# Selective scans on one Trainium2 core: taking a job's sum out and beginning the next one step apart, with additions up to three steps later

## The chip, the cores and the metric

The kernel is one program on one core of a Trainium2 chip. The metric is its device time in microseconds (us), given as the median of several executions. The core has five engines with an instruction queue each: TensorE (PE; its weight loads appear as PEld), VectorE (DVE), ScalarE (ACT), GpSimd (POOL) and SyncE (SP), which here only issues DMA transfers. They run side by side and wait for one another through semaphores.

## The reference, cut to what matters

Four layers work on an image batch of 2 x 56 x 56 x 128 in 32-bit floats. Layers 0 and 1 hold four-direction selective scans; layers 2 and 3 are attention, a spectral mixer and experts, which the change does not touch. What one scan computes, for each direction k (rows forward, columns forward, and both backward), channel d and time l:

```python
def step(state, inp):
    u_i, d_i, b_i, c_i = inp
    dA = jnp.exp(d_i[..., None] * A)
    state = dA * state + (d_i * u_i)[..., None] * b_i[:, :, None, :]
    y = jnp.einsum('bkdn,bkn->bkd', state, c_i)
    return (state, y)
```

There are 16 states n for each channel, and the output y at a time is the sum over them of state times c. The four directions are then added at each pixel. Layer 0 has 256 channels for each of two images. Layer 1 scans 64 channels of both images together, one head after another, four heads.

## The kernel before, in words

Channels lie on the 128 partitions, the 3136 pixels along the free dimension, in four quarters of 784 (`QT`). A *group* is a direction kd and a quarter q; the order of directions is 0, 2, 1, 3: rows forward, rows backward, columns forward, columns backward. A *job* is a group and a block of 128 channels (`nch` is 2 in layer 0, 1 in layer 1). A job has 16 *steps*, one for each state n. There are six runs of the scans: two of 512 steps in layer 0 (one for each image), four of 256 in layer 1 (one for each head), 2048 steps and 128 jobs in all.

For a step the work passes from engine to engine:

- ScalarE: `decay` (L334), a = exp(delta x A), into one of two PSUM buffers; `keep` (L345) saves the last column of a finished scan for the next quarter.
- TensorE: `spread` (L359) puts row n of the input matrix on all partitions, b, in a single PSUM buffer (pool `prow`). The same buffer is used by the preparation's products (L161).
- VectorE: the product h = du x b (L412), then the scan itself (L353), in place in h. For five of the 16 states (`POOLED`: 2, 5, 8, 11, 14) GpSimd makes the product (L428), from a b that a DMA has put on all partitions.
- GpSimd: the output product p = h x c (L425), with c brought by a DMA.
- TensorE: `add_up` (L373) adds p to the job's sum `acc` in PSUM with an identity matrix, two matmuls, each of which appears as two passes in the profile.

A job's sum is begun by `begin_sum` (L387): TensorE writes into `acc` what y holds for this quarter from the earlier directions, or, for kd 0, the direct term. After the 16th addition `take_out` (L393) copies `acc` back to y on ScalarE, in two copies. There is one `acc` buffer, so a job's begin waits for the take-out of the job before. `y_half` (L364) gives the place in y: for kd 1 and 3 its elements are one image row, 56 elements, apart.

The order of all instructions is written by hand: `emit(s)` issues, for every s, parts of several steps, and each engine takes its own in that order. At s it issues the decay of step s+1, `keep` of s-1, VectorE's product of s+1, the spread of s+2, a preparation's matmuls (`prepare(s, 0)`), the scan of s, the fetches of c for s+3 and of b for s+6, GpSimd's p of s and product of s+3, and then TensorE's additions. A step with n is done, for the additions, two values of s later. Before the change take_out stands first on ScalarE at the s where the new job's step 2 is scanned, and begin_sum last on TensorE at the same s; steps 0 to 7 of a job are then added three values of s after their scan, 8 to 15 two after it.

`preparation` (L252 on) makes delta, du and the bands of later groups while a job runs. Its lists give a step offset for each piece over two jobs, which I call a pair; the jobs of a pair are the first and second. In layer 0: `rows` at 0 and 3, `steps` at 12 and 16, `soft` (softplus, with a change of ScalarE's table before and after it) at 20, `copy` and `times` (du, L218) at 22 and 25. In layer 1 (after its first job): `rows` at 0 and 6, `steps` at 3 and 16, `soft` at 20, `copy` and `times` at 22 and 25. Offset 16 is step 0 of the second job. The last pair of a run has no preparation.

Of the kernel before, what the change touches and what calls it, by code (L numbers as in the profile page):

```python
# [30 lines left out]
NS = 16  # L31
# [74 lines left out]
class Scans:  # L106
# [30 lines left out]
    def open(self, ctx):  # L137
        k, nch = self.k, self.nch
        self.once = ctx.enter_context(k.pool("scan4", 1))
        self.two = ctx.enter_context(k.pool("scan5", 2))  # L140
        self.hp = ctx.enter_context(k.pool("scanh", 6))
        self.pp = ctx.enter_context(k.pool("scanp", 4))
        self.cp = ctx.enter_context(k.pool("scanc", 4))
        self.bp = ctx.enter_context(k.pool("scanb", 2))
        self.dram = ctx.enter_context(k.tc.tile_pool(name="scand", bufs=4, space=bass.MemoryType.DRAM))
        self.pa = [ctx.enter_context(k.pool(f"pdec{i}", psum=True)) for i in range(2)]
        self.pb = ctx.enter_context(k.pool("prow", psum=True))
        self.pc = ctx.enter_context(k.pool("psum", psum=True))
# [154 lines left out]
    def all_steps(self):  # L303
        steps, self.pieces = [], {}

        more = 2 // self.nch
        sets = [self.groups[:1]] + [self.groups[i : i + more] for i in range(1, len(self.groups), more)]
        for i, groups in enumerate(sets):
            for t in self.preparation(sets[i + 1], i == 0) if i + 1 < len(sets) else []:
                self.pieces.setdefault((len(steps) + t[0], t[1]), []).append(t)  # L310
            for g in groups:
                for ci in range(self.nch):
                    job = dict(g=g, ci=ci)
                    steps += [dict(job=job, g=g, ci=ci, n=n, s=len(steps) + n) for n in range(NS)]
        self.state = {}
        self.steps = steps
        for s in range(-6, len(steps) + 4):
            self.emit(s)
# [78 lines left out]
    def emit(self, s):  # L397
        nc = self.k.nc
        now, one, two, three = (self.at(s + i) for i in range(4))
        before, done, out = self.at(s - 1), self.at(s - 2), self.at(s - 3)  # L400
        if s == len(self.steps) + 2:
            self.take_out(self.steps[-1]["job"])
            return
        if out and out["n"] == NS - 1 and done:
            self.take_out(out["job"])
        if one:
            self.decay(one)
        if before:
            self.keep(before)
        if one and one["n"] not in POOLED:  # L410
            one["h"] = self.hp.tile([128, QT], F32, name="h")
            nc.vector.tensor_tensor(one["h"], one["g"]["du"][one["ci"]], one["b"], ALU.mult)  # L412
        if two and two["n"] not in POOLED:
            self.spread(two)
        self.prepare(s, 0)
        if now:
            self.scan(now)
        far = self.at(s + 6)
        if far and far["n"] in POOLED:
            far["b"] = self.on_all(self.bp, far["g"], "b", far["n"])  # L420
        if three:
            three["c"] = self.on_all(self.cp, three["g"], "c", self.w["rowC"] + three["n"])
        if now:
            now["p"] = self.pp.tile([128, QT], F32, name="p")
            nc.gpsimd.tensor_tensor(now["p"], now["h"], now["c"], ALU.mult)  # L425
        if three and three["n"] in POOLED:
            three["h"] = self.hp.tile([128, QT], F32, name="h")
            nc.gpsimd.tensor_tensor(three["h"], three["g"]["du"][three["ci"]], three["b"], ALU.mult)  # L428

        if done and done["n"] == 0:  # L430
            self.begin_sum(done["job"])
        elif done:
            if done["n"] <= 8:
                self.add_up(out)
            if done["n"] >= 8:
                self.add_up(done)
        self.prepare(s, 2)


# [1547 lines left out]
```

## Time and profile before

Times of three executions: 9255.02, 9247.24 and 9253.21 us; median 9253.21. The profiled execution took 9254.57, with a span of 9252.7.

| Engine | busy, us | share of the span |
|---|---|---|
| PE (matmul) | 8116.6 | 88% |
| DVE | 7112.8 | 77% |
| POOL | 6326.5 | 68% |
| ACT | 3840.2 | 42% |

| Scan run | first scan, us | last scan ends, us |
|---|---|---|
| layer 0, image 0 | 116.0 | 1388.8 |
| layer 0, image 1 | 1523.6 | 2795.1 |
| layer 1, head 0 | 2956.4 | 3598.4 |
| layer 1, head 1 | 3707.0 | 4345.9 |
| layer 1, head 2 | 4454.5 | 5097.2 |
| layer 1, head 3 | 5205.3 | 5844.4 |

How to read the profile's lines: a group has its line in the kernel (L412), engine and operation, out<-in, the shapes and the number of instructions; then busy us, mean ns of one, and the idle time of the engine just before them with what ended most of it. In the rows of slices each digit is the busy share of one fortieth of the span in tenths. A wait line has who waited for whom, the us in total, how often, and the longest. A timeline line has start and length in us, engine, instruction, and in brackets the engine's idle time before it and what ended it. TensorE's matmuls are pipelined and their ends are modelled, so the distance from one start to the next says more than their length.

### The profile page before, as it was taken

What the parts mean: (1) busy time and instruction counts of PE and PEld (TensorE: products, weight loads), DVE (VectorE), ACT (ScalarE), POOL (GpSimd) and SP (SyncE); (2) the same over time, 40 slices, a digit from 0 to 9 for tenths busy, and PEclk for the clock granted to TensorE, in tenths of its full rate; (3) what the DMA queues carried; (4) which work ended last, traced back from release to release, by engine and by line L of the source; (5) the groups of instructions that cost most, each with busy time, mean ns of one, the idle gap of its engine ahead of it and who ended that gap; (6) DMA issues with size and microseconds to landing.
All of it is one profiled execution on the core that took longest, in us unless ns stands there. A gap on an engine that the chain in (4) does not pass through costs nothing.

```text
span 9252.7 us, 94254 instructions
## 1 busy us (share of the span) xinstructions
PE 8116.6 (88%) x28825; PEld 4759.4 (51%) x28825; DVE 7112.8 (77%) x7587; ACT 3840.2 (42%) x6553; POOL 6326.5 (68%) x4023
## 2 busy tenths in 40 slices
PE   7888888888888888888888888599999999999998
PEld 3444445444444444444444444355588888874555
DVE  8999998999995997998899799711376676665442
ACT  4555545555544555554555555333211111114331
POOL 5999996999994996998799699666411111115551
PEclk9999999999998998999999899699999999999998
DMA  5666663666663885896688488200233333320003
GB/s 155 224 222 215 213 213 120 223 224 218 213 214 87 227 224 134 216 228 171 174 225 222 124 230 222 65 3 3 64 110 94 106 101 96 103 62 7 14 5 128
DMA packets 781381, 1364.59 MB, mean 147 GB/s; under 512 B 133213, under 2 KB 406494, under 8 KB 780842
## 3 DMA queue, kind: packets, MB, share of 16 engines
q1 hardware_dynamic: 780874, 1358.56, 51.2%
q8 instruction: 229, 3.75, 0.2%
q14 instruction: 278, 2.28, 0.1%
HBM read 1318.63 MB, written 39.60 MB: 147 GB/s over the span
## 4 chain that ended last, share of the span: by engine, by line
PE 54%; DVE 23%; issue 12%; ACT 5%; POOL 4%; DMA 1%; SPq 0%; DVEq 0%; POOLq 0%; ACTq 0%
PE cv L1515 13%; DVE h L353 11%; PE acc L373 11%; DVE h L412 7%; PE av L1027 5%; PE sc L1033 5%; PE pj L1629 4%; PE b L161 3%; PE acc L387 2%; PE b L359 2%; PE pcv L454 1%; ACT a L334 1%; POOL p L425 1%; POOL h L428 1%; PE cv L1577 1%
## 5 line engine op out<-in xcount | busy, mean ns | idle before, releaser
L425 POOL TENSOR_TENSOR p<-h,c 128x784 f32<-128x784 f32 x2048 | 3758.3, 1860 | 158.9 <-PE acc L373 91.5
L373 PE MATMUL acc<-p,ident 128*128 128x392 f32 x8192 | 3113.5, 509 | 181.3 <-POOL p L425 178.4
L353 DVE TENSOR_TENSOR_SCAN h<-a,state,h 128x784 f32<-128x784 f32 x1536 | 2794.4, 1843 | 35.7 <-POOL h L428 16.2
L373 PEld LDWEIGHTS acc<-p,ident 128*128 128x128 f32 x8192 | 1489.4, 194 | 1298.5 <-POOL p L425 372.6
L412 DVE TENSOR_TENSOR h<-du,b 128x784 f32<-128x784 f32 x1408 | 1339.6, 951 | 172.8 <-PE b L359 170.0
L334 ACT ACTIVATE a<-delta,L0A 128x784 f32<-128x784 f32 x1024 | 939.7, 919 | 864.0 <-DVE h L353 862.0
L334 ACT ACTIVATE a<-delta,L1A 128x784 f32<-128x784 f32 x1024 | 939.3, 919 | 826.8 <-DVE h L353 824.9
L428 POOL TENSOR_TENSOR h<-du,b 128x784 f32<-128x784 f32 x640 | 1188.6, 1857 | 2.9 <-DMA b<-rows 2.9
L359 PE MATMUL b<-three,sel 96*128 96x512 bf16 (+1 forms) x2816 | 703.7, 331 | 379.8 <-DVE h L412 338.6
L1046 POOL TENSOR_TENSOR total<-total,e 128x448 f32<-128x448 f32 (+1 forms) x644 | 734.4, 1140 | 326.1 <-ACT e L1035 286.4
L353 DVE TENSOR_TENSOR_SCAN h<-a,h 128x784 f32<-128x784 f32 x512 | 901.8, 1780 | 26.2 <-ACT a L334 15.5
L1528 DVE TENSOR_TENSOR u<-u,cv 128x512 f32<-128x512 f32 x1024 | 624.0, 684 | 326.5 <-PE cv L1515 325.3
L1559 POOL TENSOR_TENSOR u<-u,S 128x1024 f32<-128x1024 f32 x64 | 150.1, 2367 | 1043.8 <-DVE S L1528 1028.4
L359 PEld LDWEIGHTS <-sel 96*128 96x128 bf16 x2816 | 277.8, 99 | 974.4 <-issue 781.5
L1035 ACT ACTIVATE e<-sc 128x448 f32<-128x448 f32 (+1 forms) x700 | 376.9, 542 | 725.6 <-PE sc L1033 594.5
L1530 ACT COPY u<-cv 128x512 f32<-128x512 f32 x256 | 149.2, 586 | 827.3 <-PE cv L1515 773.7
L1629 PE MATMUL pj<-u,Wm 128*128 128x196 f32 (+8 forms) x1536 | 354.2, 384 | 5.7 <-DVE A L1635 5.7
L1033 PE MATMUL sc<-big 128*128 128x448 f32 (+1 forms) x700 | 323.5, 548 | 12.1 <-ACT e L1035 12.1
L1027 PE MATMUL av<-e,big 128*128 128x448 f32 (+1 forms) x700 | 320.8, 545 | 1.2 <-DVE e L1040 1.1
L1609 POOL TENSOR_TENSOR both<-mpm 128x512 f32<-128x512 f32 x32 | 40.6, 1269 | 390.0 <-DVE Wm L1665 271.7
L1629 PEld LDWEIGHTS pj<-u,Wm 128*128 128x128 f32 x1536 | 268.4, 192 | 71.3 <-issue 46.0
L972 DVE TENSOR_REDUCE m<-lo 112x1 f32<-112x448 f32 x392 | 229.3, 618 | 95.1 <-PE lo L968 94.9
(438 smaller groups left out, 10805.4 us busy)
## 6 DMA issues: line engine op xcount, KB each, us to landing
c<-rows SPq DMA_DIRECT2D x1024, 392.0 KB, 4.0
c<-rows SPq DMA_DIRECT2D x2048, 196.0 KB, 4.6
b<-rows SPq DMA_DIRECT2D x320, 392.0 KB, 4.6
b<-rows SPq DMA_DIRECT2D x640, 196.0 KB, 4.5
H<-raw SPq DMA_DIRECT2D x32, 1568.0 KB, 7.5
wC<-win SPq DMA_DIRECT2D x64, 576.0 KB, 6.2
w<-in_L_weight_dram SPq DMA_DIRECT2D x52, 512.0 KB, 5.3
wA<-win SPq DMA_DIRECT2D x64, 384.0 KB, 5.4
```

What stands on the lines that cost most here:

```text
L334: self.k.nc.scalar.activation(x["a"], g["delta"][ci], AF.Exp, scale=self.w["A"](g["kd"], ci, x["n"]))
L353: self.k.nc.vector.tensor_tensor_scan(h, a, h, start, ALU.mult, ALU.add)
L359: self.k.nc.tensor.matmul(ps[:, c0:c1], lhsT=self.w["selB"](x["n"]), rhs=x["g"]["three"][:, c0:c1], start=True, stop=True)
L373: nc.tensor.matmul(job["acc"][:, i, 0:392], lhsT=self.k.ident, rhs=x["p"][:, 392 * i : 392 * (i + 1)], start=False, stop=n == NS - 1,)
L412: nc.vector.tensor_tensor(one["h"], one["g"]["du"][one["ci"]], one["b"], ALU.mult)
L425: nc.gpsimd.tensor_tensor(now["p"], now["h"], now["c"], ALU.mult)
L428: nc.gpsimd.tensor_tensor(three["h"], three["g"]["du"][three["ci"]], three["b"], ALU.mult)
L1027: nc.tensor.matmul(acc, lhsT=V[b][:n, j, :], rhs=e[:n], start=j == 0, stop=j == NKT - 1)
L1033: nc.tensor.matmul(ps[:n], lhsT=keys[b][:, KT * j : KT * j + n], rhs=q, start=True, stop=True)
L1046: nc.gpsimd.tensor_tensor(total[:n], total[:n], e[:n], ALU.add)
L1515: self.k.nc.tensor.matmul(ps[:, b], lhsT=v[:, C * b : C * (b + 1)], rhs=h, start=i == 0, stop=i == len(terms) - 1)
L1629: nc.tensor.matmul(ps[:, lo - c0 : hi - c0], lhsT=Ws[f][:, eo, r, :], rhs=u[:, b, f, lo - a0 : hi - a0], start=f == 0, stop=f == 1,)
```

## The change

A finished job's take-out moves one value of s later, to where step 3 of the next job is scanned, and behind the decay instead of ahead of it. The begin of the next job's sum moves two values later, to step 4. The additions go through a list, `self.sums`: done steps are put in, the first is taken out one value of s after the begin, and at the done steps 6, 9 and 12 two are added in place of one, so that the list is empty again at the job's end. Until then an addition comes up to five values of s after its scan. The pool of output products p has six buffers in place of four.

```diff
-        self.pp = ctx.enter_context(k.pool("scanp", 4))
+        self.pp = ctx.enter_context(k.pool("scanp", 6))
...
-        self.state = {}
+        self.state, self.sums = {}, []
...
     def emit(self, s):
         nc = self.k.nc
         now, one, two, three = (self.at(s + i) for i in range(4))
-        before, done, out = self.at(s - 1), self.at(s - 2), self.at(s - 3)
+        before, done = self.at(s - 1), self.at(s - 2)
         if s == len(self.steps) + 2:
             self.take_out(self.steps[-1]["job"])
             return
-        if out and out["n"] == NS - 1 and done:
-            self.take_out(out["job"])
         if one:
             self.decay(one)
+        if done and done["n"] == 1 and done["s"] > NS:
+            self.take_out(self.at(done["s"] - 2)["job"])
         if before:
             self.keep(before)
...
-        if done and done["n"] == 0:
-            self.begin_sum(done["job"])
-        elif done:
-            if done["n"] <= 8:
-                self.add_up(out)
-            if done["n"] >= 8:
-                self.add_up(done)
+
+        if done:
+            self.sums.append(done)
+            if done["n"] == 2:
+                self.begin_sum(done["job"])
+            elif done["n"] > 2:
+                for _ in range(2 if done["n"] in (6, 9, 12) else 1):
+                    self.add_up(self.sums.pop(0))
         self.prepare(s, 2)
```

## The prediction

> **What bounds the kernel now.** I read the page's table of engines and its costliest groups first, then the clock and the waits stretch by stretch, then one job boundary in the order of time.
>
> ```profile
> DVE  8999998999995997998899799711376676665442
> POOL 5999996999994996998799699666411111115551
> ...
> L425 POOL TENSOR_TENSOR p<-h,c 128x784 f32<-128x784 f32 x2048 | 3758.3, 1860 | 158.9 <-PE acc L373 91.5
> L373 PE MATMUL acc<-p,ident 128*128 128x392 f32 x8192 | 3113.5, 509 | 181.3 <-POOL p L425 178.4
> L353 DVE TENSOR_TENSOR_SCAN h<-a,state,h 128x784 f32<-128x784 f32 x1536 | 2794.4, 1843 | 35.7 <-POOL h L428 16.2
> L412 DVE TENSOR_TENSOR h<-du,b 128x784 f32<-128x784 f32 x1408 | 1339.6, 951 | 172.8 <-PE b L359 170.0
> ```
>
> The change touches only the six scan runs (two of 512 steps, four of 256; 116 to 5844 us, with other work between them). In them VectorE works nine tenths of the time. The starts of its scans give 39.78 us for a job of 16 steps in layer 0 and 40.09 in layer 1, of which 1.43 and 1.71 are idle. So VectorE's own work is 38.4 us a job, and GpSimd's, counted the same way, is 38.7 (layer 0) and 39.1 (layer 1). Both are near their limits; what can be won is VectorE's idle time, above all the 170.0 that L412 waits for the rows that TensorE spreads. Sorted by step, 126 of these stand at one place: before the product of step 6. The waits of VectorE in the column directions (kd 1, 3) of the first run, 744 to 1389 us:
>
> ```profile
> DVE h L412 <- PE b L359: 34.7, 14, 3.4
> ```
>
> and in its row directions (kd 0, 2), 160 to 744 us:
>
> ```profile
> DVE h L353 <- ACT a L334: 5.6, 8, 0.8
> ...
> DVE h L412 <- PE b L359: 0.2, 1, 0.2
> ```
>
> So the stall belongs to jobs whose sum begins with a strided read of y. One such job, first of a pair, in the timeline (start, length, engine):
>
> ```profile
> 827.32 1.62 ACT L393 COPY pair<-acc 128x392 f32<-128x392 f32 x2 [1.56 <-PE acc L373]
> 828.99 3.13 PE L387 MATMUL acc<-pair,ident 128*128 128x392 f32 x4 [1.37 <-ACT pair L393]
> 831.94 2.79 PE L161 MATMUL b<-big,xp 128*128 128x392 f32 x4
> 834.77 0.48 ACT L173 COPY xd<-b 128x392 f32<-128x392 f32 x1 [4.09 <-PE b L161]
> 836.04 0.50 PE L359 MATMUL b<-three,sel 96*128 96x512 bf16 x2
> 836.34 1.85 POOL L425 TENSOR_TENSOR p<-h,c 128x784 f32<-128x784 f32 x1 [1.59 <-PE acc L373]
> 836.64 0.97 DVE L412 TENSOR_TENSOR h<-du,b 128x784 f32<-128x784 f32 x1 [3.37 <-PE b L359]
> ```
>
> TensorE waits for take_out, begins the sum (four passes 0.72 apart, 2.95 in all; a contiguous begin takes 1.42), makes the prepared rows, which keep the one buffer of b until ScalarE has copied them, and only then spreads step 6: the product is 3.37 late. The rows took 0.65 a pass in place of 0.33. Two stretches of this boundary (length; busy time of TensorE, its weight loads, VectorE, ScalarE, GpSimd; granted clock; DMA share; GB/s):
>
> ```profile
> 828.20:831.40 3.20, 2.41 (x4) 0.90 (x5) 3.18 (x3) 2.48 (x6) 3.20 (x3) 1.00 0.75 266
> 831.50:834.80 3.30, 3.30 (x6) 1.58 (x5) 1.77 (x2) 0.03 (x1) 3.25 (x2) 0.50 0.56 216
> ```
>
> The throttle halved TensorE's clock just there, as it does after nearly every strided begin.
>
> **What the Trainium skill says.** TensorE: Matmul & The Clock Gate, Part 1 (What's actually happening): the clock is halved after a window of about 3.4 us with too little activity, windows running freely. The trace agrees: half-clock stretches of 3.41 us, each after a window in which TensorE was mostly below half busy or read strided. SBUF — State Buffer, Door 1, note on cachelines: strided reads pay once a step leaves a 16-byte line; the trace's 0.72 against 0.33 agrees, and 0.72 stays 0.72 at half clock, so that a strided begin loses nothing to the throttle. ScalarE: Activation LUTs, What ACT_TABLE_LOAD costs: 1283 ns a load; the trace has 1283. Perfetto Trace Analysis, Optimization Strategy: a bubble that repeats can mean too few buffers; GpSimd's 91.5 for the four buffers of p are such bubbles.
>
> **The change, part by part.** In step numbers n of the new job:
>
> *take_out moves from n=2, ahead of a(3), to n=3, behind a(4).* The same two copies (next instruction 1.4 us after the first, strided). In the job above a(3) no longer waits; a(4) starts when scan(2) ends, 828.85; take_out runs 829.7 to 831.1, the state copy to 831.25. Behind it stand the copy of the rows and a(5), which must wait for scan(3)'s end (831.45) anyway. Cost nothing.
>
> *The begin moves from n=2 to n=4, behind the spread of step 6.* First of a pair: h(4) ends at 829.66, rows on TensorE at 829.7, their copy 1.63 later (as at this job's step 0) at 831.3, done 831.8; spread of 6 at 831.9; scan(4) ends at 833.27: h(6) on time with 0.7 to spare. Begin 832.25 to 835.2; spread of 7; its product can start 0.6 later, 835.8. VectorE, not delayed now, wants it at 835.9 (h(6) 0.95 and scan(5) 1.8 after 833.27). That is just in time at full clock. But TensorE does little from n=2 to 4 now (no additions), so I expect a half-clock window at or near the begin: on the rows it adds 1.31 and makes step 6 about 0.7 late, on the spread of 7 it adds 0.33. In layer 1 the preparation there is steps (copy 0.91 in place of 0.48), 0.4 tighter. Bounds 0 to 1.5; I take 0.7. Idle now at this place, from the starts sorted by job: 16 jobs each at a mean of 2.80 and 2.30 (layer 0, kd 1 and 3: 40.8 in all), 2.80 and 1.75 (layer 1: 36.4), together 77; after, 26 jobs with a preparation at 0.7, 18. Gain 59, of which GpSimd's 39.1 floor in layer 1 takes back some 0.3 in 12 jobs, 4. **55.**
>
> *Second of a pair, column directions.* No rows at n=3; spread of 6 early; begin 11.3 to 14.3 us into the same frame, spread of 7 well before h(7). But here softplus stands at n=4 on ScalarE: from scan(3)'s end 0.92 + 0.18 + 1.28 + 2 x 0.83 + 1.28 + 0.92 = 6.2 to 6.4 until a(6), against 2 x 1.78 + 2 x 0.95 = 5.5 on VectorE. That costs 0.9, as it does now in the row directions (0.21 + 0.71 a job); in the column directions the longer stall covers it. Now 44 in 32 jobs at n=4 to 6; after, 0.92 in 26, 24. **Gain 20.**
>
> *Additions three steps later, doubled at n=8, 11, 14.* The number is the same, 16 a job at 1.32 each. p(s) needs the addition of s-6, issued one step before at the earliest: no nearer than today, and later in the job three steps before, so GpSimd's waits for acc go; they are not VectorE's, except where GpSimd's late h stops a scan (22 us in the whole trace). Bounds 0 to 22 gained; I take 0. The double at n=8 (eight passes, 2.63) stands ahead of the copy at n=9 in second jobs: today TensorE begins that copy the moment h is read and du follows as scan(9) ends, without slack. Eight passes after the spread end 0.35 too late, copy-to-du latency gives back 0.1: 0.25 in 54 jobs, **loss 13.5** (0 to 22). The double at n=11 pushes steps at n=12 by 0.45 against a slack of 0.3 to 0.45 before h(15): 0.15 in 30 layer-0 jobs, **loss 4.5**. At n=14 the next spread has 0.65 to spare: nothing.
>
> *Row directions.* Begin 1.32 (2.6 at half clock) still ends before the spread of 7 is wanted; the rows may meet a half clock: 0.5 in a quarter of 28 jobs, **loss 4**.
>
> *Two more buffers of p*: other addresses in the scan pools, perhaps other waits at the six run starts; 1 us each way, taken as 0. No DMA is added or moved: c is fetched when p(s-1) is done, as before.
>
> Sum: -55 - 20 + 13.5 + 4.5 + 4 = -53. The profiled execution took 9254.57 (span 9252.7, 1.9 around it), 1.4 above the median; 9254.6 - 53 - 1.4 = **9200**.
>
> **Rivals.** *The stall only moves from step 6 to step 7* (chance 0.13): the begin's 2.95 now stands ahead of the spread of 7. If the window's half clock hits both rows and spread, first jobs stall about 2.4 in place of 0.7: 26 x 1.7 = 44 less gain, 9244. Against it: 1.75 to 2.6 us lie between the two products, which the begin did not have before. *All of it goes* (0.18): h(7) on time (18), no loss at the copies (22), less waiting for GpSimd's h (4 or so): 9156; GpSimd's floor (38.7 x 64 + 39.1 x 64 against 5112 now) allows no less than 9120. *Slower* (0.07): one mechanism, the throttle. With no additions at n=2 to 4 the low window comes in all 128 jobs, row directions too, and with a phase that puts rows, spread of 6 and the additions after them into the half clock. Its price is 1.64 (rows and spread again) less 0.7 slack, and what the backlog adds. At 0.44 us a job over the 122 jobs that have a predecessor the gain is used up, at 0.6 it is slower by 0.2%; at 1.0 a job it ends at 9322. The row directions keep 0.7 to 1.2 us of slack, which speaks against it. The likeliest course has 0.62, between 9172 and 9236.
>
> **How the numbers follow.** About 0.2% (18.5 us) is what a measurement of this kernel tells from no change. Faster by more, below 9234.7: all of "all goes" and nearly all of the likeliest, 0.79. Within it: the moved stall and a tail of the likeliest, 0.14. Slower 0.07. Range 9160 to 9245: it leaves out half of "all goes", a third of the moved stall and the slower case.
>
> **What would show it.** Right: L412's wait for L359 falls from 170 to about 70; take_out stands behind a; the begin follows the spread of 6; GpSimd's wait for acc at L373 is gone; VectorE's wait for a at n=6 grows from some 30 to some 50 us in all; du at n=9 waits for the copy; more half-clock windows at job starts. Wrong: h(7) waiting 1.5 or more, or row-direction jobs that stall at n=4 or 5.

## The result

The changed kernel takes 9184.19 us (median of 4 runs, 9174.98 to 9196.55), the kernel before 9254.11 beside it (9247.24 to 9255.53): a ratio of 0.9927, 95% interval 0.9910 to 0.9944. That is 69.9 us less, where 53 was forecast; 9184 lies inside 9160 to 9245.

The profiled execution of the changed kernel is the slowest of its four, 9196.55 with a span of 9194.7, so the two traces differ by 58.0 and not by 69.9. I divide a span into the six scan runs (from a run's first scan to the end of its last) and the rest:

| | scan runs, us | rest, us | VectorE idle in the runs, us | half clock in the runs, us |
|---|---|---|---|---|
| before | 5107.1 | 4145.6 | 200.5 | 310.7 |
| after | 5067.3 | 4127.4 | 159.6 | 493.6 |
| difference | -39.8 | -18.2 | -40.9 | +182.9 |

Half clock is the time in which the clock granted to TensorE was one half of the full one. The scan runs lose about what VectorE idles less. The other 18.2 us are outside them, and the prediction had nothing there. Of the 183 us more of half clock, 174 fall in the row directions (70 us before, 245 after), where no begin reads with a stride; the column directions had 240 us and have 249.

The costliest groups of the kernel after:

```profile
L425 POOL TENSOR_TENSOR p<-h,c 128x784 f32<-128x784 f32 x2048 | 3755.4, 1859 | 125.5 <-DVE h L353 38.6
L373 PE MATMUL acc<-p,ident 128*128 128x392 f32 x8192 | 2990.4, 499 | 23.0 <-POOL p L425 21.8
L353 DVE TENSOR_TENSOR_SCAN h<-a,state,h 128x784 f32<-128x784 f32 x1536 | 2788.5, 1837 | 48.7 <-ACT a L334 27.4
L412 DVE TENSOR_TENSOR h<-du,b 128x784 f32<-128x784 f32 x1408 | 1332.7, 947 | 96.5 <-PE b L359 91.4
```

L412 waits 91.4 us for the spread rows in place of 170.0, where the prediction had about 70. TensorE's own wait for p before an addition, 181.3, is 23.0. GpSimd's wait for `acc`, 91.5 before, was to be gone; 33.2 us remain, nearly all before p of steps 8 and 11 (9.4 and 22.2). VectorE's scans now name a (ScalarE) as their first wait, 27.4 here and 23.4 in the group of scans without a saved state. The column directions of the first run (744 to 1371 us), which had 34.7 for L412 before:

```profile
DVE h L353 <- ACT a L334: 6.0, 7, 1.1
DVE h L412 <- PE b L359: 3.4, 7, 0.8
DVE h L353 <- POOL h L428: 1.2, 5, 0.4
DVE du L218 <- PE b L161: 1.2, 6, 0.3
```

And the same job boundary as in the prediction, in the timeline of the kernel after:

```profile
832.25 1.63 ACT L393 COPY pair<-acc 128x392 f32<-128x392 f32 x2
832.28 2.00 PE L161 MATMUL b<-big,xp 128*128 128x392 f32 x4 [2.10 <-DVE h L412]
834.32 0.49 ACT L173 COPY xd<-b 128x392 f32<-128x392 f32 x1 [0.43 <-PE b L161]
834.85 0.81 PE L359 MATMUL b<-three,sel 96*128 96x512 bf16 x2 [0.57 <-ACT xd L173]
835.46 3.07 PE L387 MATMUL acc<-pair,ident 128*128 128x392 f32 x4
835.77 0.97 DVE L412 TENSOR_TENSOR h<-du,b 128x784 f32<-128x784 f32 x1
...
838.35 0.83 PE L359 MATMUL b<-three,sel 96*128 96x512 bf16 x2
839.22 0.97 DVE L412 TENSOR_TENSOR h<-du,b 128x784 f32<-128x784 f32 x1 [0.72 <-PE b L359]
```

The rows come before the begin now, the spread of step 6 (834.85) as well; its product at 835.77 has no wait. The begin stands ahead of the spread of step 7, whose product is 0.72 late. TensorE ran at half clock here too, and now idles 2.10 before the rows.

### The profile page after: what moved, and what is told of

Same layout as the page of the kernel before. It is cut to its first block, busy times and chain, and to the rows that moved or that the text cites. A ratio compares the mean times of both kernels' runs of the same rounds, so it can differ in the third digit from the quotient of the medians.

```text
span 9194.7 us, 93730 instructions
## 1 busy us (share of the span) xinstructions
PE 8062.6 (88%) x28825; PEld 4797.1 (52%) x28825; DVE 7113.2 (77%) x7587; ACT 3845.9 (42%) x6551; POOL 6325.5 (69%) x4023
## 4 chain that ended last, share of the span: by engine, by line
PE 38%; DVE 11%; issue 5%; ACT 3%; POOL 2%; DMA 1%; SPq 0%; DVEq 0%; POOLq 0%; ACTq 0%
PE cv L1516 12%; PE av L1028 6%; PE sc L1034 5%; DVE h L353 5%; PE pj L1630 4%; DVE h L412 3%; PE acc L373 2%; DMA c<-rows 1%; ACT a L334 1%; PE b L161 1%; PE cv L1578 1%; PE pcv L455 1%; POOL p L425 1%; PE every L1796 1%; PE lo L969 1%
## 5 line engine op out<-in xcount | busy, mean ns | idle before, releaser
L373 PE MATMUL acc<-p,ident 128*128 128x392 f32 x8192 | 2990.4, 499 | 23.0 <-POOL p L425 21.8
L353 DVE TENSOR_TENSOR_SCAN h<-a,state,h 128x784 f32<-128x784 f32 x1536 | 2788.5, 1837 | 48.7 <-ACT a L334 27.4
L412 DVE TENSOR_TENSOR h<-du,b 128x784 f32<-128x784 f32 x1408 | 1332.7, 947 | 96.5 <-PE b L359 91.4
L359 PE MATMUL b<-three,sel 96*128 96x512 bf16 (+1 forms) x2816 | 730.9, 342 | 572.7 <-DVE h L412 475.6
L353 DVE TENSOR_TENSOR_SCAN h<-a,h 128x784 f32<-128x784 f32 x512 | 900.7, 1777 | 33.7 <-ACT a L334 23.4
```

Of the source, the lines that this page charges most:

```text
L353: self.k.nc.vector.tensor_tensor_scan(h, a, h, start, ALU.mult, ALU.add)
L359: self.k.nc.tensor.matmul(ps[:, c0:c1], lhsT=self.w["selB"](x["n"]), rhs=x["g"]["three"][:, c0:c1], start=True, stop=True)
L373: nc.tensor.matmul(job["acc"][:, i, 0:392], lhsT=self.k.ident, rhs=x["p"][:, 392 * i : 392 * (i + 1)], start=False, stop=n == NS - 1,)
```

## The experiments

Times are medians beside fresh runs of the kernel before (9253.4 for e1 to e4, 9253.6 for e5 to e8, 9249.8 for e9 to e12). "Scan runs" is the sum from one profiled execution; steps 4, 5, 6 and so on are VectorE's idle time from just ahead of that step's scan until just ahead of the next one's, summed over all jobs. The wait before the product of step 6 therefore stands under step 4, a wait for a of step 6 under step 6. Each kernel has one profiled execution. Kernels with the same order in the scan runs, before and e1, after and e12, differ there by 2.1 and 3.6 us, so a difference of that size says nothing.

| kernel | time | ratio (95%) | scan runs | half clock | step 4 | step 5 | step 6 | 9 and 13 | layer 0 to 1 |
|---|---|---|---|---|---|---|---|---|---|
| before | 9253.4 | 1 | 5107.1 | 311 | 127.2 | 8.5 | 23.9 | under 2 each | 161.3 |
| after | 9184.2 | 0.9927 (0.9910-0.9944) | 5067.3 | 494 | 26.5 | 28.7 | 47.0 | 15.9 | 145.3 |
| e1 six buffers only | 9232.2 | 0.9978 (0.9970-0.9986) | 5109.2 | 306 | 126.1 | 9.5 | 22.5 | under 2 each | 149.8 |
| e2 begin earlier | 9270.1 | 1.0019 (1.0011-1.0026) | 5161.2 | 517 | 167.0 | 2.2 | 30.1 | 16.1 | 137.7 |
| e3 before, contiguous | 9174.3 | 0.9914 (0.9900-0.9929) | 5036.3 | 152 | 21.7 | 18.0 | 38.1 | under 2 each | 165.1 |
| e4 after, contiguous | 9186.8 | 0.9932 (0.9916-0.9949) | 5065.9 | 486 | 25.5 | 24.4 | 43.5 | 16.2 | 144.5 |
| e5 spreads 4 and 6 repeated | 9177.2 | 0.9916 (0.9902-0.9931) | 5062.7 | 193 | 29.2 | 30.0 | 39.7 | 15.9 | 138.1 |
| e6 other doubles | 9195.7 | 0.9938 (0.9923-0.9953) | 5054.1 | 573 | 24.1 | 30.0 | 44.5 | under 2 each | 155.8 |
| e7 softplus apart | 9175.3 | 0.9915 (0.9900-0.9930) | 5047.0 | 557 | 21.4 | 26.6 | 20.3 | 9.5 | 137.7 |
| e8 e6 and e7 | 9185.3 | 0.9922 (0.9906-0.9939) | 5050.2 | 585 | 24.8 | 28.6 | 16.5 | under 2 each | 150.5 |
| e9 spread 4 repeated | 9169.3 | 0.9915 (0.9898-0.9931) | 5052.8 | 326 | 8.3 | 27.6 | 41.2 | 16.0 | 139.0 |
| e10 e9 and e7 | 9149.5 | 0.9896 (0.9882-0.9911) | 5034.3 | 374 | 8.6 | 24.0 | 12.0 | 8.4 | 140.3 |
| e11 take-out earlier | 9189.5 | 0.9936 (0.9922-0.9951) | 5066.6 | 510 | 20.3 | 29.6 | 45.3 | 16.0 | 138.1 |
| e12 seven buffers | 9203.6 | 0.9953 (0.9938-0.9968) | 5070.9 | 537 | 26.0 | 30.9 | 43.8 | 15.9 | 145.8 |

The last column is the time from layer 0's last scan to layer 1's first, which I call the passage: most of what differs outside the scan runs. The intervals of the changed kernel and of most of its variants overlap, so these are compared by their scan runs and waits, not by their medians.

### What of the change does it

```diff
 (the kernel before)
-        self.pp = ctx.enter_context(k.pool("scanp", 4))
+        self.pp = ctx.enter_context(k.pool("scanp", 6))
```

> The kernel before with six buffers of output products and nothing else. If the gain comes from where take-out and begin stand (my theory): the six scan runs keep their 5107 us in all, within 5, GpSimd's 91.5 us of waiting for the accumulator shrink to under 20 and VectorE's 170 us for the spread rows stay; time 9254, unless the work between the runs is laid out differently, which can give up to 16 us as in the changed kernel (161 to 145 us between layer 0 and layer 1). If the buffers bring the gain (rival): scan runs about 5070, time about 9215 or less.

The scan runs stay (5109.2), and with them the long waits. VectorE in this kernel, and GpSimd's group:

```profile
DVE h L412 <- PE b L359: 162.4, 79, 8.5
DVE h L353 <- ACT a L334: 29.5, 40, 1.8
DVE h L353 <- POOL h L428: 25.2, 61, 1.5
...
L425 POOL TENSOR_TENSOR p<-h,c 128x784 f32<-128x784 f32 x2048 | 3757.9, 1860 | 163.3 <-PE acc L373 78.6 <-issue 25.8 <-DVE h L353 22.0
```

GpSimd's group still shows 78.6 us before p under the name of acc, where I expected under 20. Step by step these have left step 4 and stand at step 5 (28.6 us at step 4 before, none now; 34.7 at step 5, now 54.9), and in the job of the prediction p of step 5 starts 0.1 us after the scan of step 5 ends: what GpSimd waits for there is the late scan, whatever the name says. With six buffers it only reaches that scan sooner. So the prediction's reading of all the 91.5 us as too few buffers of p was right for the part at step 4 alone. Yet the kernel is 21 us faster by the medians, clear of noise, and in its trace all of the gain is outside the scan runs: 4130.3 us of rest in place of 4145.6.

```diff
 (the changed kernel)
-            if done["n"] == 2:
+            if done["n"] == 1:
                 self.begin_sum(done["job"])
```

> The changed kernel with the begin of a sum one value of s earlier, at step 3 and so ahead of the spread of step 6; additions and take-out as changed. Theory (the gain is that the strided begin no longer stands ahead of the spread of step 6): the stall before the product of step 6 returns in the column directions, about 1.7 us in first jobs of a pair, and in second jobs 1.8 in place of ScalarE's 0.9; together 50 to 85 us more than the changed kernel, 9235 to 9270. Rival (later take-out behind the decay, or the late additions, bring the gain): within 10 us of the changed kernel's 9184.

Ahead of the spread of step 6 the begin costs 94 us of scan runs and 86 us of time against the changed kernel; it is slower than the kernel before, at the upper end of what was expected. In the column directions first jobs wait 59 us at step 4 (77 in the kernel before) and second jobs 66 (40 before). The boundary, with the begin, then the spread, then the product of step 6:

```profile
839.02 3.13 PE L387 MATMUL acc<-pair,ident 128*128 128x392 f32 x4
...
841.98 0.52 PE L359 MATMUL b<-three,sel 96*128 96x512 bf16 x2
842.60 0.97 DVE L412 TENSOR_TENSOR h<-du,b 128x784 f32<-128x784 f32 x1 [1.78 <-PE b L359]
```

So later additions, more buffers and the later take-out, which are all in this kernel, bring nothing by themselves; the begin's place behind that spread does. No addition can stand ahead of its sum's begin, so the begin's move needs the later additions. Whether it needs the two more buffers as well was not run.

```diff
 (the changed kernel)
+        if done and done["n"] == 0 and done["s"] > 0:
+            self.take_out(self.at(done["s"] - 1)["job"])
         if one:
             self.decay(one)
-        if done and done["n"] == 1 and done["s"] > NS:
-            self.take_out(self.at(done["s"] - 2)["job"])
```

> The changed kernel with take-out back where the kernel before has it, at step 2 and ahead of the decay of step 3; begin and additions as changed. Theory (take-out's place costs and brings nothing, the begin's place does it all): scan runs within 12 us of 5067. Rival (take-out behind the decay is part of the gain, since a of step 3 no longer waits for TensorE's last addition): scan runs 15 us or more above, with VectorE waiting for a at step 2 or 3. Third: ScalarE is freer at step 3, and the waits at step 4 shrink by 15 us or more.

Scan runs 5066.6 against 5067.3: take-out's place is worth nothing either way, as the prediction priced it. Step 4 shrinks by 6 us, not by 15.

### What made the stall

```diff
 (e3: the kernel before; e4: the changed kernel)
-                lhsT, rhs = self.k.ident, self.y_half(job, i)
+                lhsT, rhs = self.k.ident, self.y[ci][:, QT * g["q"] + HALF * i : QT * g["q"] + HALF * (i + 1)].rearrange("p (a b) -> p a b", b=HW)
```

> The kernel before, with the begin of a sum reading the same number of elements of y in a row instead of one image row apart, for all directions but the first: so it leaves out the reordering of y and computes something else. Theory (strided begin plus the halved clock after it make the stall): the 117 us of stalls before step 6 in the column directions fall to under 20, softplus's 0.9 us shows in second jobs in their place (24 us); 70 to 85 us less, 9170 to 9184. Rival (the stall is the chain take-out, begin, rows, spread in itself, whatever the begin reads): at most 30 us less, 9225 or more.

> The changed kernel with the same contiguous read in the begin, so again without the reordering of y. Theory: the late begin has room then, and only the small waits at steps 4 and 5 of first jobs shrink; 0 to 15 us less than the changed kernel, 9169 to 9184, that is no gain over the kernel before with the contiguous read beyond what differs between the runs (16 us). Rival (the change gives something in all directions): 30 us or more below the contiguous kernel before.

VectorE in the first run's column directions, e3:

```profile
DVE h L353 <- ACT a L334: 6.2, 7, 1.0
...
DVE h L412 <- PE b L359: 2.7, 7, 0.5
```

With the contiguous read the kernel before loses 70.8 us of scan runs; the strided read with what it brings was the stall: half clock in the column directions falls with it from 240 to 69 us. The changed kernel gains 1.4 from it: its begin has room. And of the two contiguous kernels the changed one is 29.6 slower in the scan runs: 152 us of half clock have become 486, and 16.2 us of waits stand at steps 9 and 13 that were not there. So the new order has a price in all directions (17 us of VectorE's idle time in the row directions, 12 in the column directions), which the stall's end outweighs.

### What the change left behind

```diff
 (e5: the changed kernel; e9 has {4: 4})
-        for c0, c1 in ((0, 512), (512, QT)):
+        for c0, c1 in ((0, 512), (512, QT)) * {4: 4, 6: 3}.get(x["n"], 1):
             self.k.nc.tensor.matmul(
```

> The changed kernel with the spread of step 4 of each job done four times and that of step 6 three times, into the same place: more work for TensorE where the change left it idle. Theory (the halved clock makes the waits at steps 4 and 5, 55 us in all in the changed kernel): half-clock time in the scan runs falls from 494 us to under 250 and these waits by 20 to 40 us, so that the scan runs take 5027 to 5047 in place of 5067; time 9145 to 9165. Rival (the waits come from the order of TensorE's work, clock or not): the waits stay or grow by the 0.66 us that the second spread adds in some jobs, time 9184 to 9220.

> The changed kernel with the spread of step 4 of each job done four times into the same place, and nothing more (the run before repeated that of step 6 too, which costs 0.66 us just ahead of the product of step 6). Theory (the halved clock doubles the preparation's matmuls at step 3 and so delays the product of step 6): half-clock time in the scan runs well under 494 us, the waits at step 4 fall from 26.5 to under 12 us, those at step 5 by a few; scan runs 5040 to 5055 in place of 5067. Rival (those waits are ScalarE's, held up by the take-out): step 4 stays above 20 us, scan runs 5062 or more. Time 15 to 25 us below the changed kernel, apart from what the layout between the runs does, 10 us either way.

In e5 half-clock time fell to 193 us but the waits did not: 29.2 and 30.0, and the scan runs stayed at 5062.7. The timeline of a first job in layer 1 tells why. After (steps on TensorE at half clock, the product 1.09 late):

```profile
3358.70 2.56 PE L161 MATMUL b<-xd,dt 128*128 128x392 f32 x4 [2.10 <-DVE h L412]
...
3361.36 0.91 ACT L206 ACTIVATE delta<-b,L1dtb 128x784 f32<-128x784 f32 x1 [1.06 <-PE b L161]
...
3362.32 0.81 PE L359 MATMUL b<-three,sel 96*128 96x512 bf16 x2 [1.06 <-ACT delta L206]
...
3363.24 0.97 DVE L412 TENSOR_TENSOR h<-du,b 128x784 f32<-128x784 f32 x1 [1.09 <-PE b L359]
```

e9, the same job:

```profile
3342.72 1.49 PE L359 MATMUL b<-three,sel 96*128 96x512 bf16 x8
...
3345.32 1.58 PE L161 MATMUL b<-xd,dt 128*128 128x392 f32 x4 [1.11 <-DVE h L412]
...
3347.96 0.49 PE L359 MATMUL b<-three,sel 96*128 96x512 bf16 x2 [1.06 <-ACT delta L206]
...
3348.68 0.94 DVE L412 TENSOR_TENSOR h<-du,b 128x784 f32<-128x784 f32 x1
```

The preparation takes 1.58 in place of 2.56, and the product has no wait. In e5 the clock was full there as well, but the two more spreads of step 6 took their 0.66 just ahead of its product, which was 0.46 late. Without them step 4 falls to 8.3 us and the scan runs to 5052.8: the wait at step 4 is the halved clock. Step 5 stays at 27.6: 8 us for the spread of 7, behind the begin, and 18 for GpSimd's product of step 5.

```diff
 (e6: the changed kernel)
-                for _ in range(2 if done["n"] in (6, 9, 12) else 1):
+                for _ in range(2 if done["n"] in (5, 8, 12) else 1):
```

> The changed kernel with the doubled additions at the done steps 5, 8 and 12 in place of 6, 9 and 12, that is one value of s earlier for the first two, ahead of no preparation. Theory: the waits that the changed kernel has at steps 9 and 13 (10.6 and 5.3 us, du waiting for the copy and a product for its rows) go, 10 to 18 us less; scan runs 5050 to 5057, time 9166 to 9174. Rival (they come from elsewhere): no change, or the earlier doubling delays the spread of step 10 and costs 10 us.

The waits at 9 and 13 go and the scan runs lose 13.2 us, as expected. New waits stand at step 8 (5.0 us, before the product of step 10, as the rival had it) and at step 15 (10.3 us, which had none). The time does not follow (9195.7): the passage takes 155.8 us here and all that is outside the scan runs 4139.1.

```diff
 (e7: the changed kernel; the layer 0 list and the second of layer 1)
-                (16, 0, "steps", 1, [0, 1]), (20, 2, "soft", 0), (20, 2, "soft", 1), *du(22, 0), *du(25, 1),
+                (16, 0, "steps", 1, [0, 1]), (20, 2, "soft", 0), (22, 2, "soft", 1), *du(22, 0), *du(25, 1),
...
-                [(6, 0, "rows", [0, 1]), *bands(7, 13, 17, 2, 22, 31), (16, 0, "steps", 0, [0, 1]), (20, 2, "soft", 0), *du(25, 0)],
+                [(6, 0, "rows", [0, 1]), *bands(7, 13, 17, 2, 22, 31), (16, 0, "steps", 0, [0, 1]), (22, 2, "soft", 0), *du(25, 0)],
```

> The changed kernel with the second softplus of each preparation two steps later (offset 22 in place of 20), each with its own change of ScalarE's table. Theory (ScalarE's chain of two table loads and two softplus at step 4 is what second jobs now wait for at step 6, 47 us): chains of 5.4 us fit VectorE's 5.5, the wait for a at step 6 falls to under 12 us; 30 to 45 us less, time 9139 to 9154, although ScalarE loads 2.6 us more of tables for each pair. Rival (GpSimd or TensorE then stops VectorE in the same place): at most 15 us less.

> Both of the last two edits. Theory: the savings add, 40 to 60 us less than the changed kernel, 9124 to 9144, scan runs about 5015. Rival (GpSimd's floor of some 4980 us for the six runs is felt): they add to half at most, 9144 to 9165.

Step 6 falls from 47.0 to 20.3 us and the scan runs by 20.3; some of it comes back at steps 8 and 10 (10.4 and 8.8). So the chain of softplus was the wait, but less was to be had than I expected. e8, both edits: layer 0 adds them (2513.3, with one edit 2502.3 or 2502.8, with both 2492.6), layer 1 does not (2553.9, 2551.8 and 2544.2, 2557.5). The expectation failed in layer 1, and the traces show what stops it there: e6's order brings the wait at step 15, 10.3 us in e6 and 12.0 in e8, all but 0.1 of each in layer 1. One such place in e6, the end of a first job, before the product of step 1 of the next job:

```profile
3384.00 0.72 PE L359 MATMUL b<-three,sel 96*128 96x512 bf16 x2 [2.19 <-DVE h L412]
...
3384.52 4.30 PE L373 MATMUL acc<-p,ident 128*128 128x392 f32 x8
...
3388.65 0.50 PE L359 MATMUL b<-three,sel 96*128 96x512 bf16 x2
...
3389.26 0.97 DVE L412 TENSOR_TENSOR h<-du,b 128x784 f32<-128x784 f32 x1 [0.93 <-PE b L359]
```

and the same place in the changed kernel:

```profile
3385.79 0.49 PE L359 MATMUL b<-three,sel 96*128 96x512 bf16 x2 [0.89 <-DVE h L412]
...
3386.12 2.80 PE L373 MATMUL acc<-p,ident 128*128 128x392 f32 x8
...
3388.76 0.50 PE L359 MATMUL b<-three,sel 96*128 96x512 bf16 x2
...
3390.04 0.94 DVE L412 TENSOR_TENSOR h<-du,b 128x784 f32<-128x784 f32 x1
```

With two of the doublings one step earlier TensorE has less left to do here: it is busy for 0.81 us of the 3.00 before 3384.00, where the changed kernel has 2.51 of 3.40 before 3385.80. Then its clock is halved, and the doubled additions of step 14 take 4.30 us in place of 2.80 and delay the spread behind them. All 11 such waits in e6 and all 13 in e8 lie at a half-clock stretch of 3.41 us; the changed kernel has no half clock at steps 14 and 15 of layer 1. Step 8 grows in layer 1 as well, from 7.4 us in e7 to 13.6 in e8.

> The repeated spread of step 4 and the second softplus two steps later, together, on the changed kernel. If both act apart: scan runs 5020 to 5035, time 9140 to 9160, the fastest of all. If GpSimd's own work stops VectorE where the two waits go: scan runs 5040 or more, time 9165 to 9180.

e9's and e7's edits together add up: scan runs 5034.3, time 9149.5 (9139.55 to 9166.1), the lowest median here and below both, 0.9896 (0.9882 to 0.9911) of before. VectorE's waits in it:

```profile
DVE h L412 <- PE b L359: 75.1, 83, 6.9
DVE h L353 <- POOL h L428: 43.6, 81, 2.2
DVE h L353 <- ACT state L345: 14.1, 41, 0.8
DVE h L353 <- ACT a L334: 12.2, 24, 1.8
```

a has gone from 50.8 to 12.2, and GpSimd's products, 26.9 after, are 43.6. That is VectorE's largest wait inside the scan runs now; of the 75.1 for the spread rows 40.9 lie there.

### The time outside the scan runs

> The changed kernel with seven buffers of output products in place of six: the same order in the scan runs, other addresses. Theory (the 18 us that the changed kernel gains outside the scan runs come from how the work between layers 0 and 1 is ordered, which moves with the pools' size and has nothing to do with the scans): scan runs 5067, within 5; the time from layer 0's last scan to layer 1's first is not 145 but anything from 135 to 165 us, in another order of instructions. Rival (those 18 us come from the scans' new tail): 145 within 3 us, in the same order.

The edit is `"scanp", 7`. The scan runs stay within 3.6 us, but the passage is 145.8, in the same order of instructions as in the changed kernel: what the rival expected. The two passages, before and after (length, then busy TensorE, loads, VectorE, ScalarE, GpSimd, clock, DMA share, GB/s):

```profile
2795.10:2956.40 161.30, 134.10 (x552) 80.37 (x552) 75.32 (x139) 80.59 (x117) 45.04 (x45) 0.85 0.11 29
```

```profile
2761.00:2906.30 145.30, 128.44 (x548) 80.98 (x548) 74.83 (x139) 77.08 (x115) 45.51 (x52) 0.89 0.13 33
```

It is nearly the same work in 16 us less. Outside the scan runs the order is not written by hand, and I compared it engine by engine. Before and e3 have one order there (161.3, 165.1), e1 a second (149.8), the changed kernel with e2, e4, e5, e7 and e9 to e12 a third (137.7 to 145.8), e6 and e8 a fourth (155.8, 150.5). So an order goes with a time, to within 8 us. Four to six buffers changed it with the old scans, six to seven did not with the new ones, and the place of the doubled additions alone (e6, e8) changed it too. So what of the changed kernel's 16 us in the passage is the buffers' and what the new order's was not separated, and why an order is chosen stays open.

## Why the prediction was right, point by point

*The stall's place and cause.* Right, and shown: e2 brings it back, e3 takes it away without the change. That it belongs to the strided begin in the column directions, and that take-out behind the decay and the later additions cost or bring nothing alone, held (e11, e2). The reading of the clock holds over the whole kernel before: of the 86 half-clock stretches that begin in its scan runs, 36 follow 3.41 us in which TensorE was less than half busy, and the other 50 follow a strided begin. "Nearly every strided begin" is too much: 50 of 64.

*First jobs of a pair, column directions: 77 us to 18.* Measured at steps 4 and 5: 16.8. The 0.7 a job came from bounds of 0 and 1.5, and the trace has both kinds: in the job shown in layer 0 no wait at step 6's product and 0.72 at step 7's, in the one shown in layer 1 1.09 and 0.46, and others without any wait. The mean is 0.43 in layer 0 and 0.89 in layer 1, which was called 0.4 tighter. That their mixture comes out at 0.7 is in part luck. The 4 given back to GpSimd in layer 1 were 4.4: 1.8 at step 11 and 2.6 at step 14.

*Second jobs, column directions: 44 to 24.* Measured 29.2 at steps 4 to 6. ScalarE's 0.92 was right in layer 0 (0.92 a job in kd 1); layer 1 adds 0.46 at step 5 in kd 1, mostly GpSimd's product of step 5. The term was 5 too good.

*Doubled additions: 13.5 and 4.5.* Measured 10.6 at step 9 and 5.3 at step 13, and e6 takes both away. Right in place and near in size.

*Row directions: 4.* This term was wrong. First jobs there idled 23.8 before and 39.7 after; at steps 4 and 5 some 16 us more. I gave the half clock a quarter of the jobs at 0.5. In fact nearly all the half clock that the change adds is there (174 of 183 us), and 12.5 of the 26.5 us at step 4 are in the row directions' first jobs; in e9 these 12.5 fall to 2.0, so the clock makes them. A sign that had been named for being wrong, row-direction jobs that stall at step 4 or 5, thus came in part: 31.4 us there in all, 18.0 before.

*The sum.* With these the scan runs gained 40.9 of idle time against 53; the 12 between them are about what the row directions' term was too good by. The prediction omitted the 18 us outside the runs: "other addresses ... 1 us each way, taken as 0" was the step that failed. e1 shows that the edit of the buffers alone can be worth 15 us there (21 in the medians). So it was luck that 9200 lay as near to 9184 as it did: a missing gain covered a gain too large. The remaining 12 us between 58.0 (spans) and 69.9 (medians) lie in the spread of single executions, 9174.98 to 9196.55.

*The rivals.* The stall did not simply move: 28.7 us at step 5, of which 17 are waits for TensorE. The slower case named a mechanism that is there, the throttle, at several times the price that the runs show: e9, which takes away 168 of the 494 us of half clock, gets 14.5 us of scan runs back, where some 54 would have used up the gain. "All goes" is where e10 comes out, 9149.5, by two more edits.

## What to carry to other kernels

When an in-order engine stands between two others, look for the long instruction that does not need to stand ahead of the short one that somebody waits for; the waits name the short one. An edit that moves work away from TensorE can also halve its clock for the next 3.41 us, though not every gap does: of the 137 times that TensorE idles for 2 to 3 us in the changed kernel's scan runs, 84 have half clock within 3.41 us behind them. So price the work behind a gap at both clocks, in every place where the gap is made and not only where the old stall was; in e6 that place was at the other end of the job. And an edit to a pool's size can move work far from it, so compare the stretches that an edit should not touch before giving it the whole gain.

## What the runs showed of the hardware that I had not expected

A few matmuls whose result is simply written again can pay: three more spreads a job, a microsecond of TensorE, cut the half-clock time in the scan runs from 494 to 326 us and the kernel's scan runs by 14.5. Moving additions one step earlier can do the opposite, and far from the edit: the doubled additions at a job's end took 4.30 us in place of 2.80 at the halved clock (e6). And a change of ScalarE's table did not cost more than its 1.28 us in these chains: the instruction behind each of the 237 table loads in e7's scan runs (129 in the kernel after) starts 1.29 us after the load did.
